# Queries, norms and keys of the next sample made inside the last window of the layer before, values made beside the first tiles

## The chip, the cores and the metric

The kernel runs on one core of a Trainium2 chip, in one launch. The metric is device time in microseconds, the median over several executions. All arithmetic is in float32, except a split of some operands into three bfloat16 parts. The engines are named as in the profile: PE is TensorE, DVE is VectorE, ACT is ScalarE, POOL is GpSimd, and SP is the engine that issues the DMAs.

## What is computed

Four layers run over x of 4 samples, 128 channels and 64 x 64 pixels. Layer 0, the only one whose arithmetic the change moves, is an attention over the 4096 pixels of one sample, cut here to what matters:

```python
x1 = conv1x1(x, v_w, v_b)                       # values
x2 = conv1x1(x, q_w, q_b)                       # queries
weight = conv1x1(leaky(conv1x1(x2, lw1)), lw2)  # one number per pixel
bias   = conv1x1(leaky(conv1x1(x2, bw1)), bw2)
# for each sample, q = queries, v = values as (C, n):
norm   = sqrt(sum(q * q, axis=0))
k      = q / clip(norm, 1e-4)                   # keys
logits = einsum('cn,cm->nm', k, q)
mean   = logits.mean(axis=0)
sparse = relu(logits - mean * weight + bias)
attn   = softmax(logits * sparse, axis=0)
attn   = clip(attn * (sparse != 0), 1e-8)
out    = einsum('cn,nm->cm', v, attn)
y      = leaky(conv3x3(out)) + x
```

Layer 1 projects its input, runs a selective scan over the 4096 pixels (64 states for each of 128 channels) beside a depthwise convolution, and adds the result to its input. Layer 2 is another attention with scalar queries and keys, and layer 3 a selective scan in both directions over all samples together, with a group norm behind it.

## The kernel before

The samples go one after the other: `layer0(b)`, then `layer1(b)`, for b from 0 to 3. Layer 2 of sample b - 1 is done in the gaps of both (`row_weights` beside layer 0, `attend` beside layer 1), only the last sample's layer 2 has a stage of its own; layer 3 comes last.

**Layer 0** has two parts. The first, lines 355 to 392, is a loop over 8 chunks of 512 pixels. Each chunk loads x, makes the queries on PE and ACT, stores them to DRAM (`self.q0`), squares them on POOL, sums the squares on PE in two layouts, takes the roots on ACT and stores the norms to DRAM, takes the inverse norms on DVE, spreads them over the partitions on PE (`inv_ps`), multiplies them with the queries into the keys `k`, sums the keys (`ksum`), and makes the values `vT` by four PE products and one DVE addition. The instructions of this loop are free for the scheduler to arrange. The mean of the keys follows, and `thresholds(0)`: four PE products one after the other with ACT and DVE steps between them, from the queries to the cut `ncut` and the bound `bound` of a block of 512 queries.

The second part, lines 591 to 637, is a loop over 128 tiles, 16 for each of the 8 blocks of queries. A tile makes 256 x 512 logits (`lg`) from keys and queries on PE; DVE adds the cut (`above`) and multiplies (`weights`), POOL subtracts the bound, ACT takes exp (`shifted`); masking is done on DVE for even tiles and on POOL for odd ones (`masked`). Eighteen tiles later (`LAG` = U + 2) the weights get their floor (`floored`) and meet the values (`product`), so the values aren't read in the first 18 tiles. Through `self.pinned()` every instruction of this part keeps its program order on its engine. Smaller jobs, the thresholds of the next block, the normalization and the convolution of finished blocks, are lists of steps in a `Queue`; each tile takes up to two of them and one that begins on PE.

**Layer 1** cuts the 4096 pixels in 4 windows of 1024. A window has 64 items (16 groups of 8 channels for each of 4 groups of states), so a sample has 256; all go through one `scan_stream`. An item loads a row of decays (`row<-d`, 512 KB broadcast from DRAM, asked for three items ahead), makes exp on ACT, spreads the driving term on PE, multiplies it on DVE, runs a scan on DVE and a product on POOL; four items later PE sums the products (`total`). Every fourth item has its driving term made on POOL instead. Beside the items, `side(k, n)` takes steps from a queue with `queue.tile`: one that begins on PE (not at every fourth item), and up to two others, where a step marked `on_dve` is held back till just before the next item's scan (`queue.late`). In windows 0 to 2 the queue holds the preparation of the next window (`prepared`: projection, norm, steps, with stores and loads over DRAM), in all windows the depthwise convolution of the window and the end of the window before it (`finish`). The end of the last window (`finish(3)`) runs after the last item: the last `total`, the output projection, the residual `res` and the first pass of layer 2.

Layer 0 of the next sample begins after this end: its first load waits until the last store of layer 1, `x2` from `res`, is over, since it takes the memory of layer 1's tiles.

Of the kernel before, what the change touches and what calls it, by code (L numbers as in the profile page):

```python
# [8 lines left out]
F32 = mybir.dt.float32  # L9
# [20 lines left out]
class Queue:  # L30
# [11 lines left out]
    def first(self, *runs):  # L42
        self.runs[:0] = [list(r) for r in runs]
# [72 lines left out]
class Net:  # L116


    def __init__(self, ctx, tc, ins, out):
# [178 lines left out]
    def weights12(self):  # L298
# [32 lines left out]
    def layer0(self, b):  # L331
# [8 lines left out]
        with self.pool("l0", 1) as big, self.pool("l0t", 2) as tmp, self.pool("l0a", LAG + 3) as ap, \  # L340
# [3 lines left out]
            ypad = self.padded_image(big, "ypad")  # L344
            ksum = big.tile([P, NCH], F32, name="ksum", tag="ksum")
            def misc(name, rows=P):
                return ps1.tile([rows, NB], F32, name=name, tag="misc")
# [6 lines left out]

            for c in range(NCH):
                s = bass.ts(c, NB)
# [45 lines left out]
            queue = Queue()  # L402
            held = {}
            qs, ncut, bound = {}, {}, {}

# [176 lines left out]
            beside = self.row_weights(b - 1, big, tmp) if b else lambda i: None  # L582
            queue.add(thresholds(0))
            queue.steps(1)
            if b == 0:
                self.weights12()
            logits(0)
            logits(1)
            above(0)
            due = {}  # L590
            for i in range(S + LAG + 2):
# [35 lines left out]
                if i < S and m == 1 and c + 1 < NCH:  # L627
                    queue.add(thresholds(c + 1))

# [231 lines left out]
    def layer1(self, b):  # L861
# [12 lines left out]
        with self.pool("l1", 1) as big, self.pool("l1c", 2) as work, self.pool("l1t", 2) as tmp, \  # L874
# [238 lines left out]
            def depthwise(w):  # L1113
# [31 lines left out]
                return steps  # L1145

            blocks, begins, runs = [], [], []
            for w in range(NW):
# [24 lines left out]
            def before(k, n):  # L1173
# [667 lines left out]
```

## Time and profile before

| | us |
|---|---|
| median of 3 runs | 10780.06 |
| lowest and highest of them | 10776.46, 10784.34 |
| profiled execution | 10792.41 |
| span of the profiled execution | 10790.6 |
| layer 0 tiles of the four samples, first to last e | 68.6 to 687.7, 1767.8 to 2407.8, 3505.9 to 4143.5, 5239.8 to 5877.3 |
| layer 1 items, first to last scan | 817.9 to 1681.0, 2535.7 to 3422.0, 4272.7 to 5157.5, 6005.2 to 6879.0 |
| layer 2 of the last sample begins | about 6891 |
| granted PE clock, mean | 0.893 |

Times inside the profiled execution count from the first instruction. A row of the timeline has the start, the duration, the engine, the line, the operation, output and inputs, and how many instructions were merged; in brackets stands how long the engine had been idle and what ended that. Line L111 is a helper through which all pinned instructions go, so those are told apart by their tiles. SPq rows are the issuing of DMAs. A row of the table by stretches has the stretch, its length, and for each engine the time that it was busy with the number of its instructions, then the granted PE clock, the busy share of the DMA engines and the rate that they moved.

### The profile page before, as it was taken

To read this page: it belongs to the slowest core of one execution; us is meant where nothing else is said; L and a number is where in the kernel's file an instruction comes from. 1 tells how busy PE (TensorE), PEld (TensorE's weight loads), DVE (VectorE), ACT (ScalarE), POOL (GpSimd) and SP (SyncE) were. 2 spreads that over 40 slices of the span, in tenths; PEclk is the share of its full clock that TensorE was granted. 3 is DMA by queue.
4 is the path that set the end of the run, shared out by engine and by line. 5 is a ranking of instruction groups with operands and counts; after the bars stand their busy time and mean duration, and the time that the engine had idled before them with its cause. 6 is when DMAs were issued, how large, how long until landed. Compare 5 with 4: busy or idle time off the path is not lost. (4 is left out here: it accounts for less than half of the span.)

```text
span 10790.6 us, 91073 instructions
## 1 busy us (share of the span) xinstructions
PE 8558.2 (79%) x28025; PEld 3043.4 (28%) x28104; DVE 9230.7 (86%) x6438; ACT 6291.6 (58%) x9435; POOL 8141.7 (75%) x3566
## 2 busy tenths in 40 slices
PE   8986667997877897877799778787777777777774
PEld 3331212332222333222233222332222222222221
DVE  7859996986997885999787799529999999999996
ACT  3324444664664664666465566556666666676764
POOL 6748886765886774888675688429999999998986
PEclk9997778998998998999899899889988898888887
DMA  1008772006885002788100788338888888888886
GB/s 29 15 20 195 191 191 58 12 15 149 206 201 147 10 15 68 198 204 201 40 17 12 176 210 198 94 73 205 197 208 196 209 198 209 208 225 224 223 218 179
DMA packets 502953, 1522.34 MB, mean 141 GB/s; under 512 B 83433, under 2 KB 91145, under 8 KB 502465
## 3 DMA queue, kind: packets, MB, share of 16 engines
q1 hardware_dynamic: 502464, 1516.51, 56.7%
q8 instruction: 223, 3.65, 0.2%
q14 instruction: 266, 2.17, 0.1%
HBM read 1327.38 MB, written 125.94 MB: 135 GB/s over the span
## 5 line engine op out<-in xcount | busy, mean ns | idle before, releaser
L111 POOL TENSOR_TENSOR p<-h,c_rep 128x1024 f32<-128x1024 f32 x2048 | 4807.3, 2357 | 818.6 <-DVE h L111 766.4
L111 DVE TENSOR_TENSOR_SCAN h<-da,carry,db 128x1024 f32<-128x1024 f32 x1536 | 3604.1, 2346 | 201.5 <-ACT da L111 22.4
L111 PE MATMUL db<-parts,sel 96*128 96x512 bf16 x4096 | 1404.9, 429 | 1546.6 <-DVE h L111 1527.4
L111 DVE TENSOR_TENSOR db<-b_rep,db 128x1024 f32<-128x1024 f32 x1536 | 1855.2, 1208 | 199.1 <-DMA b_rep<-bc 133.4
L111 ACT ACTIVATE da<-row,A 128x1024 f32<-128x1024 f32 x1536 | 1760.9, 1147 | 305.8 <-DMA row<-d 302.5
L111 POOL TENSOR_TENSOR e<-e,bound 128x1024 f32<-128x1024 f32 x512 | 1240.5, 2425 | 566.6 <-DVE e L111 566.4
L111 POOL TENSOR_TENSOR x<-row,b_rep 128x1024 f32<-128x1024 f32 x512 | 1209.1, 2362 | 151.8 <-DMA row<-d 151.0
L111 PE MATMUL total<-p,gather 128*32 128x512 f32 x8192 | 1256.5, 729 | 19.6 <-POOL p L111 19.6
L111 DVE TENSOR_TENSOR_SCAN h<-db,carry,x 128x1024 f32<-128x1024 f32 x512 | 1194.7, 2333 | 73.8 <-ACT db L111 43.7
L111 ACT ACTIVATE db<-db,A 128x1024 f32<-128x1024 f32 x512 | 555.5, 1085 | 1194.7 <-PE db L111 1139.7
L111 PEld LDWEIGHTS <-sel 96*128 96x128 bf16 x4096 | 307.3, 101 | 3119.9 <-DVE h L111 2151.6
L111 ACT ACTIVATE e<-e 128x1024 f32<-128x1024 f32 x512 | 541.0, 1057 | 1050.0 <-POOL e L111 1050.0
L111 PE MATMUL lg<-q,k 128*128 128x512 f32 x2048 | 1027.3, 626 | 153.1 <-DVE e L111 152.6
L111 PE MATMUL acc<-t,vT 128*128 128x512 f32 x2048 | 956.2, 594 | 6.4 <-DVE t L111 3.3
L111 PE MATMUL acc<-e,values 128*128 128x512 f32 x1536 | 856.2, 648 | 87.1 <-ACT e L111 61.5
L111 DVE TENSOR_TENSOR t<-lg,ncut 128x1024 f32<-128x1024 f32 x512 | 624.9, 1220 | 292.6 <-PE acc L111 260.7
L111 ACT ACT_TABLE_LOAD x593 | 760.8, 1283 | 39.5 <-DMA r<-y 18.9
L111 ACT COPY carry<-h 128x1 f32<-128x1 f32 x2048 | 374.6, 185 | 554.0 <-DVE h L111 549.8
L111 ACT ACTIVATE e<-gq,below,fcol 128x512 f32<-128x512 f32 x768 | 610.0, 805 | 94.8 <-PE acc L111 94.8
L111 POOL TENSOR_TENSOR t<-t,e 128x1024 f32<-128x1024 f32 x256 | 608.9, 2379 | 47.5 <-ACT t L111 45.9
L111 ACT ACTIVATE junk<-gp,ntop,fcol 128x512 f32<-128x512 f32 x768 | 619.5, 807 | 27.1 <-DMA gp<-g 14.4
L111 DVE SCALAR_TENSOR_TENSOR e<-t,lg 128x1024 f32<-128x1024 f32 x512 | 619.5, 1210 | 2.5
(214 smaller groups left out, 10007.9 us busy)
## 6 DMA issues: line engine op xcount, KB each, us to landing
row<-d SPq DMA_DIRECT2D x2048, 512.0 KB
parts<-split SPq DMA_DIRECT2D x960, 64.0 KB
b_rep<-bc SPq DMA_DIRECT2D x96, 512.0 KB
c_rep<-bc SPq DMA_DIRECT2D x96, 512.0 KB
d<-delta SPq DMA_DIRECT2D x80, 384.0 KB
r<-y SPq DMA_DIRECT2D x48, 512.0 KB
xq<-in_x SPq DMA_DIRECT2D x64, 256.0 KB
q<-q SPq DMA_DIRECT2D x64, 256.0 KB
```

The source lines that it names most:

```text
L111: return self.tc.keep_in_program_order(method(*args, **kwargs))
```

## The change

For samples 1 to 3 the first loop of layer 0 is gone. In its place `layer1(b)` for b < 3 gets a list of steps, `tokens(b + 1)`, which joins the queue when its last window begins. It works in 4 pieces of 1024 pixels: it loads x, makes queries and their squares on ACT from one PE product, the norms on PE and ACT, the inverse norms on DVE, the spreading on PE, the keys on DVE and the sums of the keys on ACT (`accum_out` into `self.ksum`, now a tile that lives through the whole kernel); queries, keys and norms are stored to DRAM, the keys into a new array `self.k0`. What is left in the queue at the last item is run there. It borrows layer 1's tiles: `delta` and `du` for queries, `res` for squares, `u` for keys, `split` for the small ones.

Layer 0 of samples 1 to 3 begins with the load of the first block's queries and norms, then 8 loads of keys, and the thresholds. Sample 0 keeps its first loop, without the values. The values of all samples become eight runs of three steps in the queue (`values`: load, four products, addition), taken in the first tiles; the thresholds of the second block go ahead of them. The weights `lin_wT` are asked for behind the first thresholds, and `W_inc` is made in place.

```diff
+        self.k0 = dram.tile([P, L], F32, name="k0", tag="k0")
+        self.ksum = self.const.tile([P, NCH], F32, name="ksum", tag="ksum")
-        self.W_inc = pool.tile([P, P], F32, name="W_inc", tag="W_inc")
+        self.W_inc = self.W_in[:, 0:P]
 # layer0
-            for c in range(NCH):
+            def key(c):
+                s = bass.ts(c, NB)
+                sp.dma_start(out=k[:, s], in_=self.k0[:, s])
+
+            for c in range(0 if b else NCH):
...
-                ps = misc("v_ps").rearrange("p (a b) -> p a b", b=P)
-                for i in range(4):
-                    nc.tensor.matmul(ps[:, i, :], xq[:, bass.ts(i, P)], self.v_wT, start=True, stop=True)
-                nc.vector.tensor_tensor(
-                    vT[:, 4 * c : 4 * c + 4, :], ps,
-                    self.v_b.unsqueeze(1).to_broadcast([P, 4, P]), ALU.add,
-                )
-            self.load_all(big, ["lin_wT"])
+            def values(c):
+                def load():
+                    held["xv"] = row("xq")
+                    sp.dma_start(out=held["xv"], in_=self.ins["x"][b, :, bass.ts(c, NB)])
+                def v():
+                    held["v"] = misc("v_ps").rearrange("p (a b) -> p a b", b=P)
+                    for i in range(4):
+                        pe.matmul(held["v"][:, i, :], held["xv"][:, bass.ts(i, P)], self.v_wT, start=True, stop=True)
+                def plus():
+                    dve.tensor_tensor(
+                        vT[:, 4 * c : 4 * c + 4, :], held["v"], self.v_b.unsqueeze(1).to_broadcast([P, 4, P]), ALU.add,
+                    )
+                return [load, on_pe(v), plus]
...
             queue.add(thresholds(0))
+            if b:
+                queue.step()
+                for c in range(NCH):
+                    key(c)
             queue.steps(1)
+            self.load_all(big, ["lin_wT"])
...
+            for c in range(NCH):
+                queue.add(values(c))
             logits(0)
...
-                    queue.add(thresholds(c + 1))
+                    (queue.add if c else queue.first)(thresholds(c + 1))
 # layer1
+            def tokens(b):
+                M = W // P
+                held, small = {}, []
+                def load(u):
+                    held["x", u] = work.tile([P, W], F32, name="x", tag="x")
+                    sp.dma_start(out=held["x", u], in_=self.ins["x"][b, :, bass.ts(u, W)])
+                def first():
+                    small.append(tmp.tile([P, 3, NB], F32, name="split", tag="split", bufs=1))
+                    load(0)
+                def a(u, c):
+                    def go():
+                        held["ps"] = misc("q_ps")
+                        pe.matmul(held["ps"], self.q_wT, held["x", u][:, bass.ts(c, NB)], start=True, stop=True)
+                    return on_pe(go)
+                def query(u, c):
...
+                        act.activation(held["q", u][:, s], held["ps"], AF.Identity, bias=self.q_b)
+                        act.activation(held["sq"][:, s], held["ps"], AF.Square, bias=self.q_b)
+                def squares(u):
...
+                                held["ps"][:, i : i + 1], held["sq"][:, bass.ts(i, P)], self.ones[:, 0:1],
...
+                def root(u):
+                    def go():
+                        act.activation(norm(u), held["ps"][:, 0:M], AF.Sqrt)
+                        self.exp_tables(act)
+                    return go
+                def inverted(u):
+                    def go():
+                        dve.tensor_scalar(inverse(u), norm(u), 1e-4, None, ALU.max)
+                        dve.reciprocal(inverse(u), inverse(u))
+                    return go
+                def turned(u):
...
+                        pe.matmul(held["ps"][:, 0:P], norm(u), self.ident, start=True, stop=True)
+                def kept(u):
+                    return lambda: act.copy(as_rows(u), held["ps"][:, 0:P])
+                def spread(u, c):
...
+                def key(u, c):
...
+                        dve.tensor_tensor(held["k", u][:, s], held["ps"], held["q", u][:, s], ALU.mult)
+                    return on_dve(go)
+                def store(u):
+                    def go():
+                        t = bass.ts(u, W)
+                        sp.dma_start(out=self.q0[:, t], in_=held["q", u])
+                        sp.dma_start(out=self.k0[:, t], in_=held["k", u])
+                        sp.dma_start(out=self.norms[:, t].rearrange("o (i p) -> (o i) p", p=P), in_=as_rows(u))
+                    return go
+                def sums(u):
...
+                            act.activation(
+                                small[0][:, 2, :], held["k", u][:, bass.ts(c, NB)], AF.Identity,
+                                accum_out=self.ksum[:, u * C + c : u * C + c + 1],
+                            )
+                steps = []
+                for u in range(NW + 1):
+                    if u < NW:
+                        beside = ([sums(u - 2)] if u > 1 else []) + ([lambda u=u: load(u + 1)] if u + 1 < NW else [])
+                        steps += [a(u, 0), query(u, 0), then(*beside), a(u, 1), query(u, 1)]
+                    else:
+                        steps += [sums(u - 2)]
+                    if u:
+                        steps += [inverted(u - 1), turned(u - 1), kept(u - 1)]
+                        for c in range(C):
+                            steps += [spread(u - 1, c), key(u - 1, c)]
+                    if u < NW:
+                        steps += [squares(u), root(u)]
+                    if u:
+                        steps += [store(u - 1)]
+                return first, steps + [sums(NW - 1)]
...
                     queue.add(image(w) + depthwise(w))
+                    if w == NW - 1 and not last:
+                        first, steps = tokens(b + 1)
+                        first()
+                        queue.add(steps)
                 queue.tile(i % 4 != 1)
+                if i == NW * SG * G - 1:
+                    queue.late()
+                    while queue:
+                        queue.step()
```

More of the change, by code (lines that the diff above doesn't have):

```diff
@@ L344, in layer0 @@
             ypad = self.padded_image(big, "ypad")
-            ksum = big.tile([P, NCH], F32, name="ksum", tag="ksum")
+            ksum = self.ksum
             def misc(name, rows=P):
@@ L1145, in depthwise, with norm, inverse, as_rows @@
                 return steps
+            def tokens(b):
[14 more added lines that the diff above has]
+                    def go():
+                        s = bass.ts(c, NB)
+                        if c == 0:
+                            held["q", u] = scratch(("delta", "du")[u % 2])
+                            held["sq"] = scratch("res")
+                        act.activation(held["q", u][:, s], held["ps"], AF.Identity, bias=self.q_b)
[3 more added lines that the diff above has]
+                    def go():
+                        held["ps"] = misc("n_ps")
+                        for i in range(M):
+                            pe.matmul(
+                                held["ps"][:, i : i + 1], held["sq"][:, bass.ts(i, P)], self.ones[:, 0:1],
+                                start=True, stop=True,
+                            )
+                    return on_pe(go)
+                def norm(u):
+                    return small[0][:, 0, 2 * u * M : (2 * u + 1) * M]
+                def inverse(u):
+                    return small[0][:, 0, (2 * u + 1) * M : (2 * u + 2) * M]
+                def as_rows(u):
+                    return small[0][0:M, 1, bass.ts(u, P)]
+                def root(u):
[4 more added lines that the diff above has]
+                def inverted(u):
+                    def go():
+                        dve.tensor_scalar(inverse(u), norm(u), 1e-4, None, ALU.max)
+                        dve.reciprocal(inverse(u), inverse(u))
+                    return go
+                def turned(u):
+                    def go():
+                        held["ps"] = misc("t_ps", M)
+                        pe.matmul(held["ps"][:, 0:P], norm(u), self.ident, start=True, stop=True)
+                    return on_pe(go)
+                def kept(u):
+                    return lambda: act.copy(as_rows(u), held["ps"][:, 0:P])
+                def spread(u, c):
+                    def go():
+                        held["ps"] = misc("i_ps")
+                        for i in range(NB // P):
+                            pe.matmul(
+                                held["ps"][:, bass.ts(i, P)],
+                                inverse(u)[:, c * NB // P + i : c * NB // P + i + 1].to_broadcast([P, P]),
+                                self.ident, start=True, stop=True,
+                            )
+                    return on_pe(go)
+                def key(u, c):
+                    def go():
+                        s = bass.ts(c, NB)
+                        if c == 0:
+                            held["k", u] = work.tile([P, W], F32, name="u", tag="u")
+                        dve.tensor_tensor(held["k", u][:, s], held["ps"], held["q", u][:, s], ALU.mult)
+                    return on_dve(go)
+                def store(u):
+                    def go():
+                        t = bass.ts(u, W)
+                        sp.dma_start(out=self.q0[:, t], in_=held["q", u])
+                        sp.dma_start(out=self.k0[:, t], in_=held["k", u])
+                        sp.dma_start(out=self.norms[:, t].rearrange("o (i p) -> (o i) p", p=P), in_=as_rows(u))
+                    return go
+                def sums(u):
+                    def go():
+                        for c in range(C):
+                            act.activation(
+                                small[0][:, 2, :], held["k", u][:, bass.ts(c, NB)], AF.Identity,
+                                accum_out=self.ksum[:, u * C + c : u * C + c + 1],
+                            )
+                    return go
+                def then(*fs):
+                    def go():
+                        for f in fs:
+                            f()
+                    return go
+                steps = []
[7 more added lines that the diff above has]
+                        steps += [inverted(u - 1), turned(u - 1), kept(u - 1)]
+                        for c in range(C):
+                            steps += [spread(u - 1, c), key(u - 1, c)]
[4 more added lines that the diff above has]
+                return first, steps + [sums(NW - 1)]
```

## The prediction

> **What bounds the kernel now.** I read the page's engine rows first, to see that no single engine fills the span; then the timeline at the three joints where layer 1 of one sample hands over to layer 0 of the next; then the table by stretches, to see what bounds the two places that receive the moved work; then single timeline rows for the price of what is new. The chain of waits on the page is empty here, so the path is read from the timeline.
>
> ```profile
> span 10790.6 us, 91073 instructions
> PE 8558.2 (79%) x28025; PEld 3043.4 (28%) x28104; DVE 9230.7 (86%) x6438; ACT 6291.6 (58%) x9435; POOL 8141.7 (75%) x3566
> ```
>
> The time is a string of stages with different limits; VectorE at 86% is a mean over them. The joint before the second sample:
>
> ```profile
> 1703.16 0.42 SPq L111 DMA_DIRECT2D x<-res  x1
> 1705.97 0.81 SPq L358 DMA_DIRECT2D xq<-in_x  x2
> 1709.25 2.04 PE L360 MATMUL lg<-xq,q_wT 128*128 128x512 f32 x2 [6.95 <-DMA xq<-in_x]
> 1752.68 1.59 PE L111 MATMUL th_ps<-q,w_T 128*64 128x512 f32 x2 [0.86 <-DMA q<-q]
> 1762.71 5.69 PE L111 MATMUL lg<-q,k 128*128 128x512 f32 x8
> ```
>
> Line 1 stores layer 1's last piece, line 2 loads x for the new sample as soon as that store is over, line 3 is the first query product. For 43 us the queries, norms, keys and values are made with nothing beside them (line 4 ends that), then the threshold chain runs, and the attention tiles begin on line 5. The same distance from line 3 to line 5 is 53.46 us here, 52.16 at the next joint (3448.99 to 3501.15) and 52.19 at the last (5182.74 to 5234.93): 157.8 us in all. Stretches (layer-1 windows 1, 2 and 3 of the second sample, and above them the first 16 tiles of its layer 0):
>
> ```profile
> core 0: us, PE busy (x) PEld busy (x) DVE busy (x) ACT busy (x) POOL busy (x), PEclk, DMA share, GB/s
> 1767.80:1842.00 74.20, 50.97 (x130) 14.98 (x128) 57.67 (x43) 48.44 (x84) 59.04 (x24) 0.88 0.00 0
> 2759.30:2981.50 222.20, 179.73 (x646) 64.28 (x646) 215.60 (x137) 149.11 (x228) 188.82 (x82) 0.91 0.83 207
> 2981.50:3207.60 226.10, 180.25 (x661) 65.42 (x661) 215.89 (x137) 153.92 (x235) 188.96 (x82) 0.95 0.81 200
> 3207.60:3424.40 216.80, 161.06 (x559) 50.12 (x558) 210.79 (x132) 118.68 (x187) 185.36 (x81) 0.86 0.71 176
> ```
>
> The last window, where the new work goes, has room on ScalarE, TensorE and the DMA queue, but VectorE is busy 210.8 of 216.8 us: what is added there on VectorE is paid. The first tiles have 16 us free on VectorE out of 74, but as gaps in a chain.
>
> **Part 1, taken off the joints.** At the joint the changed program loads queries, norm rows and keys from DRAM and goes straight to the threshold chain; the means of the keys come from sums held in SBUF. The first load can start where line 2 starts, since the same store of layer 1 is awaited. I let the chain's first product begin where the first query product begins now. The chain then costs 10.0 us at this joint (1752.68 to 1762.71) and 8.8 at the last. Here a rule weighs in: the Trainium skill, "TensorE: Matmul & The Clock Gate", Part 1, says that TensorE halves its clock after about 3.4 us of idleness and needs as much work to get it back. The removed products are what kept it warm. The first sample shows a chain that is cold all through:
>
> ```profile
> 53.36 1.97 PE L111 MATMUL th_ps<-q,w_T 128*64 128x512 f32 x2
> 61.77 2.07 PE L111 MATMUL th_ps<-h,bw_rep 64*128 64x512 f32 x2 [0.84 <-DVE m L111]
> ```
>
> From 53.36 to the first tile product at 63.77 it is 10.4 us. By the rows of the joints themselves the gain would be 157.8 - (10.0 + 8.8 + 8.8) = 130.2; by the rule and the cold row 157.8 - 3 x 10.4 = 126.6. I take **-126.6** (bounds -134 and -118). The key loads are 8 x 256 KB; only the first is needed by the first tile, the others at two tiles each (9.5 us), so they hide behind the tiles; lin_wT is loaded at 1694.82 before and stays near there.
>
> **Part 2, added to three last windows.** Per window, with durations of like rows:
> - VectorE: 8 key products like k<-inv_ps,q at 0.69: 5.5 us. 4 reciprocals of 0.18: 0.7. 4 clamps of 128x8 (tensor_scalar, SBUF to SBUF): 0.16 each when alone, but see below.
> - ScalarE: 8 x (0.69 + 0.60) for queries and squares, 8 x (0.69 + 0.19) for the sums, 4 roots of 0.27 with two table loads of 1.28, 4 small copies: 30 us.
> - TensorE: 8 query products as pairs (8 x 1.0), 32 of the norm, 32 of the spreading at 0.25 to 0.29, 4 turns: 26 us.
> - SP and DMA: 4 loads of 512 KB, 8 stores of 512 KB and 4 of 4 KB: 6.3 MB on the 38 MB that pass now (176 GB/s by 216.8 us), so 205 GB/s, what windows 1 and 2 carry.
>
> ScalarE would reach 149, TensorE about 187: windows 1 and 2 run with as much and take 222 to 226. So these engines are bounded by a row, and the window should become a little worse than those, by what VectorE has more. The clamp's price:
>
> ```profile
> 2841.42 0.66 DVE L111 TENSOR_TENSOR u<-u,rs_ps 128x512 f32<-128x512 f32 x1
> 2841.64 2.35 POOL L111 TENSOR_TENSOR p<-h,c_rep 128x1024 f32<-128x1024 f32 x1 [1.25 <-DVE h L111]
> 2842.12 2.43 DVE L111 TENSOR_SCALAR u<-u,gamma,beta 128x1024 f32<-128x1024 f32 x1
> ```
>
> The tensor_scalar takes 2.43 where it takes 0.81 with GpSimd idle (776.62), and ends just after GpSimd's product; a PSUM source (first row) isn't touched. "GPSIMD Engine Reference", 1. Specifications, has the rule: GpSimd shares its SBUF interfaces with VectorE and collides with two-port or two-input instructions. By the short row alone the 4 clamps cost 0.6; by rule and row up to 4 x 1.8 = 7.2. The clamp stands right after a scan, when GpSimd is often just free, so I take 1.0 each, 4.0. VectorE: 5.5 + 0.7 + 4.0 = 10.2. Windows with side work also idle more (6.6 and 10.2 against 6.0): +2.3. So 12.5 a window, **+37.5** for three (bounds 21 and 56).
>
> A second rule speaks against the roots: "ScalarE: Activation LUTs", What ACT_TABLE_LOAD costs, gives 2.66 us a switch, a drain included, thus 5.3 for root and back. The trace has load 2827.65, root 2828.95, load 2829.23, next work 2830.53: 2.9 us with no drain to be seen. The rule would add 11 us of ScalarE a window, 160 of 229: still not the bound, nothing in the sum.
>
> **Part 3, the end of layer 1.** The queue is drained at the last item. In the changed order only the last turn, two spreads, two key products, the three stores and two pairs of sums are left there. They lie in VectorE's 6.25 us wait for the last total. But the residual load res<-x, issued at 1657.48 now, comes behind the last key store on SP, some 3.7 us after the last scan's end; with an estimated 4 us to land (the x store's 2.8 and the keys ahead) it meets its use 9.6 us after that end. On one PSUM bank the second spread waits for the first key product and holds the last totals back by about half a microsecond. +1 each, **+3** (0 to 9).
>
> **Part 4, values beside the first tiles.** 32 loads move into SP's order behind the keys, 32 VectorE additions of 0.69 and 128 products move into the tiles. In samples two to four a pair of tiles takes 9.5 us (starts of e<-t,lg 2.45 and 7.05 apart), chained from VectorE's e through GpSimd and ScalarE's exp back to VectorE's masking; an addition stands after each masking, so it lengthens the chain by up to 8 x 0.69 = 5.5 us a sample, or nothing where it falls in a wait. I take 5: **+15** (0 to 17). The first v product is queued behind six tile products; 2.75 MB stand before its x, 14 us at 200 GB/s, landing at 1722 against its turn at about 1727: hidden, 1 us each for each microsecond later.
> In the first sample the value products leave the prologue (5.4 us a chunk; without the 0.7 of v products and the addition before the clamp an estimated 4.5): -7. The weights' loads hold SP there (21.6 us for the A_log pieces), so tile products queue behind the first value load; with the additions +5. **-2** (-8 to +6).
>
> Sum: -126.6 + 37.5 + 3 + 15 - 2 = -73.1. The profiled execution took 10792.4 (span 10790.6 and 1.8 around it), 12.4 above the median of 10780.1; on the median's base 10707, in a profile about 10719.
>
> **The rivals.**
> - Cheap landing (14%): additions and clamps fall into waits. Windows +7 each, values 0, tail 0: -126.6 + 21 - 7 = -113, 10667. Against it: VectorE idles only 6 us in the window.
> - Late start (15%): loads or the drain lie in the way after all; 8 us a joint for a v product stuck behind slow key loads (98 GB/s was the mean of the old prologue), or for the residual. -73 + 24 = -49, 10731. Against it: the store of line 1 moved 512 KB within 2.8 us.
> - Slower (3%): the key store waits on SP for VectorE, and the row<-d loads are queued behind it. A row is asked for three items, 10 us, ahead; when a store holds SP longer than that lead less the landing, ScalarE's decay and the scan stop. 12 stores lose the whole gain at 73 / 12 = 6.1 us each; at 8 us the time is 10803. Against it: the store's step comes a full tile after its key product; in windows 1 and 2 of the third sample row loads were waited for only 2.4 us, beside as many bytes.
> - The work is moved and nothing gained (3%): the joint's wait is the store of line 1 and a chain as long as before; 10780. Against it: lines 3 to 5.
> - The forecast has the other 65%.
>
> The range 10668 to 10742 takes the forecast with its bounds, most of the cheap case and the late start. Under 0.2% (21.6 us) is about what a measurement of this kernel can't tell from no change. Faster 0.94, within it 0.03, slower 0.03.
>
> **What would show it.** Right: about 10.4 us from the first th_ps to the first lg at each joint, th_ps starting some 6 us after the x store; last windows of 225 to 230 us with VectorE near 221; the first 16 tiles about 5 us longer; clamps between 0.2 and 2.4. Wrong: a joint above 20 us, a last window above 236, SP waiting in a key store with a row wait behind it, or first tiles no longer than now.

## The result, and the profile after

The changed kernel takes 10659.3 us (median of 5 runs, 10649.1 to 10665.2) against 10779.1 for the kernel before (5 runs, 10776.3 to 10784.3): ratio 0.9888, 95% interval 0.9873 to 0.9902. It is faster by 120 us where the prediction said 73, and lies 9 us below the lower end of the range. The direction was right, the size wrong.

The page's head, to compare with the head shown before:

```profile
span 10662.4 us, 91085 instructions
PE 8514.6 (80%) x28080; PEld 3044.8 (29%) x28080; DVE 9216.5 (86%) x6390; ACT 6331.1 (59%) x9504; POOL 8117.2 (76%) x3542
```

Nothing in it shows where 120 us went, since the shares moved by a point at most. The joint before the second sample does (timeline; start, duration, engine, line, operation):

```profile
1703.12 0.42 SPq L111 DMA_DIRECT2D x<-res  x1
1705.90 0.32 SPq L111 DMA_DIRECT2D q<-q  x1
...
1708.82 1.94 PE L111 MATMUL th_ps<-q,w_T 128*64 128x512 f32 x2 [6.55 <-DMA own<-norms]
...
1719.32 2.93 PE L111 MATMUL lg<-q,k 128*128 128x512 f32 x3
```

The store of layer 1's last piece is followed at once by the load of the queries, and the threshold chain starts 5.7 us after the store was issued. Before, that store was followed by 43 us of queries, norms, keys and values. (The wait is put down to the norms' load, issued 0.4 us behind that of the queries; the product reads the queries.) The chain itself takes 10.50 us.

The stretches that the prediction rested on, after the change (the second sample's first 16 tiles, then its layer-1 windows 1 to 3, counted from 0):

```profile
core 0: us, PE busy (x) PEld busy (x) DVE busy (x) ACT busy (x) POOL busy (x), PEclk, DMA share, GB/s
1724.00:1797.30 73.30, 55.28 (x194) 22.20 (x192) 63.41 (x52) 48.45 (x84) 59.10 (x24) 0.93 0.07 22
2712.40:2936.10 223.70, 178.11 (x647) 62.66 (x646) 215.82 (x137) 148.77 (x228) 188.98 (x82) 0.93 0.83 206
2936.10:3162.10 226.00, 184.22 (x661) 66.64 (x660) 216.14 (x138) 152.96 (x236) 189.24 (x82) 0.92 0.81 200
3162.10:3382.40 220.30, 172.48 (x699) 68.79 (x698) 215.56 (x147) 143.55 (x232) 185.56 (x81) 0.93 0.78 197
```

In the first row VectorE carries 5.7 us more than before (63.41 against 57.67), yet the 16 tiles are no longer (73.30 against 74.20, and 72.60 in a second profile of the kernel before). In the last row VectorE carries 4.8 us more (215.56 against 210.79), and the window is 3.5 us longer.

Stage by stage, from the starts of the same instructions in each trace. The third column is a second profile of the kernel before, the first experiment below. Sums over samples, in us:

| stage | before | before, again | after | after less before | forecast |
|---|---|---|---|---|---|
| three joints, last scan's end to first tile product | 231.2 | 233.2 | 99.7 | -131.5 | -123.6 (parts 1 and 3) |
| three last windows | 645.6 | 645.6 | 659.1 | +13.5 | +37.5 (part 2) |
| first 16 tiles, samples 2 to 4 | 219.5 | 217.9 | 219.1 | -0.3 | +15 (part 4) |
| first sample up to its 16th tile | 135.2 | 135.2 | 136.3 | +1.1 | -2 (part 4) |
| layer 0's last tile to layer 1's first scan | 515.1 | 507.2 | 505.9 | -9.2 | 0 |

The first four rows give -117.2, close to the 119.8 between the medians. The last row looked like a gain that nobody had foreseen; it isn't one.

### The profile page after: what moved, and what is told of

It reads as the page before. It is cut to its first block, busy times and chain, and to the rows that moved or that the text cites. A ratio compares the mean times of both kernels' runs of the same rounds, so it can differ in the third digit from the quotient of the medians.

```text
span 10662.4 us, 91085 instructions
## 1 busy us (share of the span) xinstructions
PE 8514.6 (80%) x28080; PEld 3044.8 (29%) x28080; DVE 9216.5 (86%) x6390; ACT 6331.1 (59%) x9504; POOL 8117.2 (76%) x3542
## 5 line engine op out<-in xcount | busy, mean ns | idle before, releaser
L111 PE MATMUL total<-p,gather 128*32 128x512 f32 x8192 | 1251.2, 730 | 10.4 <-POOL p L111 10.2
L111 ACT ACT_TABLE_LOAD x617 | 791.6, 1283 | 38.9 <-DMA r<-y 17.6
```

What stands on the lines that cost most here:

```text
L111: return self.tc.keep_in_program_order(method(*args, **kwargs))
```

## The experiments

**The kernel before, profiled again.**

> The kernel before, unchanged, for a second profile. It tells how much one stage differs between two profiles of the same program. Theory A (the stretch from layer 0's last tile to layer 1's first scan, 124 to 128 us in the changed kernel and 127.8 to 130.2 in the one before, is shorter by 1.5 to 3.9 us a sample only because TensorE's granted clock fell otherwise in that execution): at least two of the four stretches move by 1 us or more, some below 127. Theory B (the change shortens it): all four within 0.5 us of 130.2, 127.8, 129.2 and 127.9. The last windows (213.5, 216.7, 215.4, 215.1) should move by less than 1.5 us, the joints (79.4, 76.8, 75.1 from the last scan's end to the first tile product) by less than 1. Time ratio 1.000.

Span 10772.5 us against 10790.6 in the first profile, ratio 1.0007 (0.9998 to 1.0015). The stretch of the last row moves by 7.9 us in sum between two profiles of one program; in the changed kernel TensorE's granted clock from 90 to 110 us behind the last tile of the fourth sample is 0.74, in the first profile of before 0.59. So the -9.2 is mostly the spread between executions. Theory A holds, and differences of some 8 us in that row mean nothing: over the 14 profiles of all runs it lies between 497.2 and 515.1. The last windows repeat within 1.4 us each, the joints within 1.3.

The runs below leave most stages of the changed kernel as they are, and so show how much a stage varies from one execution to the next. Unaltered, the joints give 98.3 to 100.4 (4 profiles), the last windows 659.1 to 663.5 (5), the first 16 tiles of samples 2 to 4 219.1 to 223.1 (5), and the first sample up to its 16th tile 133.7 to 136.4 (5). So the row of the joints is firm, that of the last windows is +13.5 to +18, and the two rows of the first tiles can't be told from nothing. Within a last window VectorE's busy time repeats to 0.4 us. Its idle time does so only in the first sample (4.7 to 5.1); in the second and third it goes from 4.5 to 7.1 in the changed kernel and from 4.7 to 6.3 before.

**Are VectorE's additions in the last window paid?** Each key product is issued twice.

```diff
                 dve.tensor_tensor(held["k", u][:, s], held["ps"], held["q", u][:, s], ALU.mult)
+                dve.tensor_tensor(held["k", u][:, s], held["ps"], held["q", u][:, s], ALU.mult)
```

> The changed kernel with each of the 24 moved key products on VectorE (0.67 us) issued twice. Theory A (the forecast's: what is added to VectorE in the last window is paid at its row duration or more, with more idle time): the three last windows grow by 5 us or more each, +15 to +20 in all. Theory B (VectorE is one closed chain there; an added instruction is paid at its step from start to start, and nothing else comes with it): 7 more in the window at 0.55 to 0.6, so +3.9 to +4.2 a window, +12 in all, idle time unchanged at about 4.7. Theory C (the additions fall into waits): below +1 a window. Against the kernel before: 0.9888 in theory C, 0.990 in B, 0.9905 in A; the windows in the profile decide, not the ratio.

The three last windows:

```profile
1456.20:1678.80 222.60, 150.06 (x604) 55.41 (x604) 217.63 (x149) 107.33 (x177) 185.34 (x81) 0.79 0.72 183
3149.60:3375.40 225.80, 176.68 (x699) 69.87 (x698) 219.83 (x153) 143.39 (x231) 185.84 (x81) 0.91 0.76 192
4858.10:5084.70 226.60, 184.01 (x699) 72.37 (x698) 219.62 (x153) 143.46 (x231) 185.88 (x81) 0.87 0.75 191
```

They are 4.4, 5.5 and 6.0 us longer than in the changed kernel (218.2, 220.3, 220.6). Six more products stand in each, and VectorE is busy 3.9 to 4.3 us more, 0.7 each; the rest is idle time of 0.2, 1.2 and 2.1 us. The ratio is 0.9907 (0.9892 to 0.9921). Theory C falls: these additions find no wait. B has the busy time right. The added idle time that A foresaw is not shown: the 5.0, 6.0 and 7.0 us here lie within what unaltered windows have.

**What does the clamp cost?** Clamp and reciprocal are put one place later.

```diff
                 dve.reciprocal(inverse(u), inverse(u))
-            return go
+            return on_dve(go)
```

> The changed kernel with the clamp and the reciprocal put one place later on VectorE: not right behind a scan but behind the next item's product db<-b_rep,db. Theory A (the clamp, SBUF to SBUF, cannot go on while GpSimd's product runs, and was cheap, 0.15 to 0.38 us, only because it stood in the gap of 0.3 us between two GpSimd products): it now takes 0.9 to 2.2 us each, ending with GpSimd's product, and the last windows grow by about 1 us for each of the 3 or 4 clamps in them, 2 to 5 us a window. Theory B (a clamp of 8 columns is cheap wherever it stands): 0.15 to 0.4 each, windows within 1 us of 218.2, 220.3 and 220.6.

Timeline of the changed kernel, then of this one, at the same clamp:

```profile
3324.20 2.33 DVE L111 TENSOR_TENSOR_SCAN h<-db,carry,x 128x1024 f32<-128x1024 f32 x1
3324.43 4.67 POOL L111 TENSOR_TENSOR p<-h,c_rep 128x1024 f32<-128x1024 f32 x2 [1.26 <-DVE h L111]
3326.44 0.38 DVE L111 TENSOR_SCALAR split<-split 128x8 f32<-128x8 f32 x1
3326.85 0.20 DVE L111 RECIPROCAL split<-split 128x8 f32<-128x8 f32 x1
```

```profile
3332.06 1.21 DVE L111 TENSOR_TENSOR db<-b_rep,db 128x1024 f32<-128x1024 f32 x1
3332.36 2.35 POOL L111 TENSOR_TENSOR p<-h,c_rep 128x1024 f32<-128x1024 f32 x1
3333.18 1.57 DVE L111 TENSOR_SCALAR split<-split 128x8 f32<-128x8 f32 x1
3334.67 2.35 POOL L111 TENSOR_TENSOR x<-row,b_rep 128x1024 f32<-128x1024 f32 x1
3334.78 0.20 DVE L111 RECIPROCAL split<-split 128x8 f32<-128x8 f32 x1
```

Below, the clamp starts amid GpSimd's product and ends with it (3334.75 against 3334.71); above, it starts as one GpSimd product has 0.35 us to go (the row merges two; the first ends at 3326.79) and slips through before the next. Over the twelve clamps it is 0.15 to 0.38 us above and 1.42 to 1.57 below. The last windows grow by 4.1, 4.6 and 6.7 us, of which VectorE's busy time is 4.4, 4.7 and 4.6; the ratio is 0.9908 (0.9893 to 0.9923). Theory A holds: the price belongs to the place. The product db<-b_rep,db, which reads PSUM, isn't touched in the same lines (1.21 us; 1.207 is its mean).

**Are the value additions paid?** Each is issued twice.

```diff
                 dve.tensor_tensor(
                     vT[:, 4 * c : 4 * c + 4, :], held["v"], self.v_b.unsqueeze(1).to_broadcast([P, 4, P]), ALU.add,
                 )
+                dve.tensor_tensor(
+                    vT[:, 4 * c : 4 * c + 4, :], held["v"], self.v_b.unsqueeze(1).to_broadcast([P, 4, P]), ALU.add,
+                )
```

> The changed kernel with each of the 32 moved value additions on VectorE (0.68 us) issued twice. Theory A (the forecast's: an addition after each masking lengthens the chain of a pair of tiles): the first 16 tiles of a sample grow by 8 x 0.6 = about 5 us, +19 in all. Theory B (GpSimd and the waits around it set the pair's 9.51 us, and the addition fills time in which VectorE would have waited or been held up): 73.3, 72.6 and 73.3 us of samples 2 to 4 stay within 0.7, and a pair of tiles stays at 9.5 us. Ratio to the kernel before 0.9905 in A, 0.9888 in B.

Samples 2 to 4 take 74.4, 73.3 and 73.3 us (73.3, 72.6, 73.3 without), and a pair of tiles stays at 9.51 to 9.53 us: theory B there, with one value 1.1 us up instead of 0.7, which unaltered runs show too (74.9). In the first sample a pair goes from 7.96 to 8.39 us, and the 16 tiles from 71.1 to 78.1. So the additions aren't free everywhere. Three such pairs make 1.3 of those 7 us. Another 3.0 lie around one late threshold step (TensorE waits 2.69 us for ScalarE's m); the run with the values alone has that step late by as much in its first sample (2.5 us) with no addition doubled, so it can't be put down to them. The cause of that, and of the rest, is open. The ratio is 0.9890 (0.9874 to 0.9907).

**What does set the pair?** One of ScalarE's two row-weight exponentials per tile is issued twice in the first 16 tiles.

```diff
-            act.activation(junk, g[0], AF.Exp, ...)
+            for _ in range(2 if i < 16 and u % 2 == 0 else 1):
+                act.activation(junk, g[0], AF.Exp, ...)
```

> The changed kernel with one of the two row-weight exponentials on ScalarE (junk<-gp, 0.80 us and 0.19 for its sum) issued twice in each of the first 16 tiles of samples two to four. Theory A (a pair of tiles goes round between GpSimd and ScalarE, 9.51 us, and VectorE stands outside of that ring, so that the doubled value additions cost nothing): the pair grows by 1 to 2 us, the first 16 tiles by 6 to 15 us a sample. Theory B (VectorE's masking and products set the pair): within 1 us of 73.3, 72.6 and 73.3.

In the one execution of this run the pair is 10.45 us instead of 9.51 and the 16 tiles 78.8 us in each of samples 2 to 4: +17.2 in sum. That is 0.94 for the pair and 5.5 to 6.2 for a sample, just under theory A's ranges and far from B; of two added ScalarE steps of 0.99 us a pair, one lies on the ring. The ring, in the changed kernel's timeline (GpSimd and ScalarE rows and VectorE's masking of one pair):

```profile
3458.85 0.81 ACT L111 ACTIVATE junk<-gp,ntop,fcol 128x512 f32<-128x512 f32 x1
3459.66 1.04 ACT L111 ACTIVATE t<-t 128x1024 f32<-128x1024 f32 x1
3460.61 1.04 ACT L111 ACTIVATE e<-e 128x1024 f32<-128x1024 f32 x1
3460.78 2.36 POOL L111 TENSOR_TENSOR t<-t,e 128x1024 f32<-128x1024 f32 x1 [1.51 <-ACT t L111]
3461.68 2.55 DVE L111 SCALAR_TENSOR_TENSOR t<-t,e 128x1024 f32<-128x1024 f32 x1 [1.25 <-ACT e L111]
3463.10 3.34 POOL L111 TENSOR_TENSOR e<-e,bound 128x1024 f32<-128x1024 f32 x1
3464.15 0.68 DVE L111 TENSOR_TENSOR vT<-v_ps,v_b 128x512 f32<-128x512 f32 x1
3466.40 2.37 POOL L111 TENSOR_TENSOR e<-e,bound 128x1024 f32<-128x1024 f32 x1
```

GpSimd waits 1.51 us for ScalarE's t, which stands behind the row-weight exponential; then GpSimd runs its three products in a row, and ScalarE's next exponential (3466.48) waits for the second of them. VectorE's e and its addition aren't on the ring: its e for the next tile was ready at 3459.29, 3.8 us before GpSimd took it up at 3463.10, and even the other e of the pair, made behind the addition (3464.75, 1.20 us), is ready some 0.4 us before GpSimd's last product of the row begins. That product isn't on the ring either: it ends at 3468.77, and ScalarE takes its result at 3470.12. The addition takes slack, and the wait of 1.25 us ahead of the masking shows that VectorE has it. The masking itself may be on the ring: the GpSimd product that begins beside it takes 3.34 us, the like one behind it 2.37. That the masking holds it up was not tested.

**The values alone.** The kernel before with only the values moved.

> The kernel before with only the values moved beside the first tiles; queries, norms and keys are made at the joint as before. By the theory that the additions stand in waits of the tiles (first 16 tiles of samples two to four longer by under 1 us), the gain is what leaves the four prologues: about 0.7 us of products and additions for each of 8 chunks where they set the pace; the first sample's prologue became 3.3 us shorter in the changed kernel. So each joint 2.5 to 4 us shorter, the first sample's tiles 4.5 us longer from the late load: -5 to -10 us, ratio 0.9990 to 0.9995. By the forecast's own terms (+5 a sample in the tiles) it would be no gain or a loss of up to 10.

A miss: 10778.5 against 10773.4 us, ratio 1.0004 (0.9996 to 1.0013). The joints are 237.9 us in sum, longer than before, not shorter. Four chunks of queries and keys with the values beside them (before), and without them (this kernel):

```profile
3463.20:3481.60 18.40, 18.35 (x111) 12.48 (x112) 8.51 (x20) 5.47 (x12) 3.13 (x4) 1.00 0.31 102
```

```profile
3453.20:3471.90 18.70, 16.74 (x80) 9.27 (x80) 10.20 (x16) 5.38 (x13) 4.15 (x4) 1.00 0.25 87
```

A chunk takes 4.68 us before and 4.66 here (query products at 42.78, 47.46 and 52.15 us behind the last scan before, at 43.35, 48.01 and 52.66 here). TensorE shows busy all the time in the first row, and taking 1.14 us of value products out of each chunk changes nothing. In this kernel TensorE waits in the first joint 3.2 us for GpSimd's square and 3.0 for VectorE's reciprocal (0.9 and 1.5 before); that these hand-overs set the pace is how I read it, no run tests it. Without the values the threshold chain is slower (31.1 us in sum against 27.6). So moving the values alone is worth nothing; the gain comes with the queries, norms and keys. What these would bring with the values left at the joint was not run.

**Why did the end of layer 1 not get longer?** The kernel before with spare products at its last item.

```diff
                 queue.tile(i % 4 != 1)
+                if i == NW * SG * G - 1 and not last:
+                    while queue:
+                        queue.step()
+                    for _ in range(2):
+                        ps = misc("i_ps")
+                        for m in range(NB // P):
+                            pe.matmul(ps[:, bass.ts(m, P)], self.ones, self.ident, start=True, stop=True)
```

> The kernel before with 8 spare TensorE products (128x128, result unused) at the last item of layer 1 of the first three samples, where the changed kernel has the drained products of the keys. Theory A (these products keep TensorE's clock up, which is why the end of layer 1 got shorter and not longer in the changed kernel): the four output products after the last scan take 2.0 instead of 3.8 us, and the first query product comes about 2 us sooner after the last scan's end (25.9, 24.6 and 22.9 now), -4 to -6 us in all. Theory B (the 2 us come from another order of the stores): distances as before within 0.7.

The output products behind the last scan: before, with the spare products, and in the changed kernel, where the drained spreads of the keys stand ahead of them.

```profile
3431.89 3.78 PE L111 MATMUL o_ps<-xc,W_out 128*128 128x512 f32 x4 [1.31 <-DVE xc L111]
```

```profile
3406.67 2.27 PE L111 MATMUL i_ps<-ident,ones 128*128 128x128 f32 x16
...
3417.31 1.98 PE L111 MATMUL o_ps<-xc,W_out 128*128 128x512 f32 x4 [1.31 <-DVE xc L111]
```

```profile
3383.03 1.16 PE L111 MATMUL i_ps<-ident,split 128*128 128x128 f32 x8 [1.99 <-DVE u L111]
...
3389.66 1.98 PE L111 MATMUL o_ps<-xc,W_out 128*128 128x512 f32 x4 [1.31 <-DVE xc L111]
```

With the spare products the first query product comes 22.2, 21.2 and 21.1 us behind the last scan, not 25.9, 24.6 and 22.9: -9.0 in all, more than theory A's -4 to -6, because the last totals quicken too (o_ps starts 5.8 us behind the scan, not 7.5). The queue that the edit drains was empty: the traces differ in these products alone. The granted clock over o_ps is 0.50 in the first of the three fences and 1.00 in the other two. Chance has a part: in the third joint of the kernel before o_ps took 1.98 without help (3.78 at all three in the second profile), and in one joint of the run with the queries kept it took 3.67 in spite of the drained spreads. The time falls by too little for a verdict (0.9994, 0.9987 to 1.0001).

**Is the chain at the joint slow for the clock?** The changed kernel with 16 spare products in TensorE's wait for the queries.

```diff
                 for c in range(NCH):
                     key(c)
+                for _ in range(4):
+                    ps = misc("w_ps")
+                    for m in range(NB // P):
+                        pe.matmul(ps[:, bass.ts(m, P)], self.ones, self.ident, start=True, stop=True)
```

> The changed kernel with 16 spare TensorE products (128x128, result unused) ahead of the threshold chain of samples two to four, in the 5.4 us in which TensorE waits for the queries from DRAM. Theory A (the chain of 10.50 us runs on a clock that went down in that wait): the chain falls to about 8.8 us, what it was behind the query and value products in the kernel before, -1.7 us a joint, -5 in all. Theory B (the chain's length comes from the hand-overs between engines): 10.3 to 10.5 as now. If the spare products last longer than the wait, the chain starts later by the difference.

The third joint, with them:

```profile
5084.48 4.70 PE L111 MATMUL w_ps<-ident,ones 128*128 128x128 f32 x32
5090.56 1.04 PE L111 MATMUL th_ps<-q,w_T 128*64 128x512 f32 x2 [1.38 <-issue]
5092.50 1.12 PE L111 MATMUL th_ps<-q,kbar_rep 128*128 128x512 f32 x2 [0.90 <-ACT h L111]
5094.30 1.12 PE L111 MATMUL th_ps<-h,lw_rep 64*128 64x512 f32 x2 [0.68 <-ACT m L111]
5096.27 1.12 PE L111 MATMUL th_ps<-h,bw_rep 64*128 64x512 f32 x2 [0.84 <-DVE m L111]
```

The chain is 6.76 us here, 8.30 at the second joint, and still 10.50 at the first. The stretches of the chain at the first joint of the changed kernel and at the third here have granted clocks (third figure from the end) of 0.50 and 1.00:

```profile
1708.80:1719.30 10.50, 8.06 (x8) 1.77 (x8) 0.75 (x1) 1.27 (x2) 0.00 (x0) 0.50 0.88 304
```

```profile
5090.50:5097.30 6.80, 4.32 (x8) 1.08 (x8) 0.75 (x1) 1.27 (x2) 0.00 (x0) 1.00 0.99 353
```

At the second joint it is 0.75. So the clock is worth up to 3.7 us of the chain. Ratio 0.9882 (0.9867 to 0.9897), not apart from the changed kernel's.

Why only one of three joints stays fast can be read from the clock's own record. In all 14 profiles the granted clock is 0.50 or 1.00, and its changes (over 600 in each) lie whole multiples of 3.41 us apart, all but one in a hundred of them to 0.002 us. So it moves only at the ends of fixed slots of 3.41 us. In this run it fell at the end of these slots, one for each joint:

```profile
1697.60:1701.01 3.41, 1.61 (x13) 1.23 (x11) 1.64 (x9) 0.00 (x0) 0.00 (x0) 1.00 0.45 148
3400.85:3404.26 3.41, 1.84 (x4) 0.59 (x4) 0.00 (x0) 1.27 (x2) 0.00 (x0) 1.00 0.89 295
5093.86:5097.27 3.41, 2.12 (x4) 0.59 (x4) 0.75 (x1) 0.39 (x1) 0.00 (x0) 1.00 1.04 389
```

That is just ahead of the chain at the first joint, in its third product at the second, and as it ended at the third. Once down, the clock came back only behind slots in which TensorE was at least 79% busy (all 4381 rises of the 14 profiles, with the ends of products as the profile models them); the slots of the first joint's chain are 62 to 80% busy, 2.11 to 2.74 us, and it stayed at 0.50. Falls mostly follow emptier slots (under 77% busy in 95% of them), but a slot of 1.76 us at the second joint let the clock stay up, so the busy share alone does not decide a fall.

**The first sample's late load.** x for the first values is loaded ahead of the later layers' weights.

```diff
+            runs = [values(c) for c in range(NCH)]
             if b == 0:
+                runs[0].pop(0)()
                 self.weights12()
-            for c in range(NCH):
-                queue.add(values(c))
+            for run in runs:
+                queue.add(run)
```

> The changed kernel with the first sample's first load of x for the values issued ahead of the weights of the later layers, not behind them. In the changed kernel TensorE stands 7.3 us in the first tiles (68.5 to 75.8), waiting for that load, which is issued at 72.40 when the A_log pieces are through. Theory A (that wait is paid): the first 16 tiles of the first sample go from 71.1 to about 66.5 us, the time falls by 4 to 5 us. Theory B (the next loads behind the weights, q and own norms of the second chunk at 72.86 and 73.28, hold the tiles as long): 70 to 71 us, nothing gained. Other samples unchanged.

The first value product in the changed kernel and here:

```profile
75.78 2.04 PE L111 MATMUL v_ps<-v_wT,xq 128*128 128x128 f32 x8 [7.32 <-DMA xq<-in_x]
```

```profile
68.33 1.05 PE L111 MATMUL v_ps<-v_wT,xq 128*128 128x128 f32 x8
```

The 7.32 us wait is gone, and the 16 tiles take 67.0 us, not 71.1: theory A. The ratio, 0.9882 (0.9866 to 0.9899), is not apart from the changed kernel's.

**The first queries kept in SBUF.**

```diff
                 act.activation(held["q", u][:, s], held["ps"], AF.Identity, bias=self.q_b)
+                if u == 0 and c == 0:
+                    act.activation(self.q_first, held["ps"], AF.Identity, bias=self.q_b)
...
-                qs[c] = held["q"] = row("q")
-                sp.dma_start(out=qs[c], in_=self.q0[:, s])
+                if b and c == 0:
+                    qs[c] = held["q"] = self.q_first
+                else:
+                    qs[c] = held["q"] = row("q")
+                    sp.dma_start(out=qs[c], in_=self.q0[:, s])
```

> The changed kernel with the first 512 queries of the next sample kept in SBUF by one more ScalarE copy of 0.69 us in the last window, so that the joint loads no queries before its threshold chain; for room the mean column is 1 wide, and two replicated weight columns are read with stride 0. Theory A (the load of the queries, issued behind the last store of layer 1 and landing about 3 us later, is what the joint ends on): the chain starts about 4 us sooner after the last scan's end (23.5, 22.2 and 22.5 now), so -12 us in all, and up to 1.7 us more a joint where TensorE's clock is then still up; the time falls by 0.11 to 0.16%. Theory B (the release of layer 1's buffers behind its last stores is what it ends on): the chain starts within 1 us of now.

The chain starts 18.5, 16.7 and 16.6 us behind the last scan's end, 5.0 to 5.9 us sooner; the joints are 82.1 us in sum, -17.6. Theory A. Ratio 0.9873 (0.9859 to 0.9888).

**Both together, without and with spare products in the chain.**

> Two edits of the runs before together on the changed kernel: the first 512 queries of the next sample stay in SBUF, and the first sample's first load of x for the values is issued ahead of the later layers' weights. If each keeps its gain (17.6 us at the three joints, 4.1 in the first tiles, both read from stages), the time falls by 20 to 22 us below the changed kernel's, 10630 to 10640 us, ratio to the kernel before 0.987. If the gains are taken back later (other stages vary by some 8 us in sum from one profile to the next), 10650.

> The same two edits, and 22 spare TensorE products (128x128, result unused) in the waits of the threshold chain of samples two to four: 14 behind its first product, 4 behind the second, 4 behind the third. Theory A (the last two products of the chain, 1.1 to 2.1 us each in the run with the queries kept, are long because TensorE's clock falls in the waits between them): all four take about 1.1, and the way from the first product to the first tile product (11.74, 9.49, 9.15) shortens by about 1.2 us each. Theory B (the hand-overs set it, and the spare products stand in the way): unchanged or longer by up to 1 us.

Without: 10638.8 us against 10773.4 for the kernel before on the same chip, ratio 0.9874 (0.9857 to 0.9890). By stages against the changed kernel the joints give -18.3 and the first sample -4.2; the last windows take back 3.9, which is within their spread. The intervals of the two ratios overlap, so the stages, not the ratio, say that it is the faster of the two. Its second joint:

```profile
3380.53 1.07 PE L111 MATMUL th_ps<-q_first,w_T 128*64 128x512 f32 x2
3381.46 0.42 SPq L111 DMA_DIRECT2D x<-res  x1
3383.09 0.68 ACT L111 ACTIVATE h<-th_ps,w_b 64x512 f32<-64x512 f32 x1 [1.96 <-DMA h<-values]
3383.92 1.10 PE L111 MATMUL th_ps<-q_first,kbar_rep 128*128 128x512 f32 x2 [2.33 <-DVE kbar_rep L176]
```

The chain now starts ahead of layer 1's last store; its second step waits for layer 1's store of the values, whose memory h seems to take. With the spare products all four products take 1.0 to 1.1 us as theory A says, but the 14 behind the first one last 3.4 us, past that wait: the chain takes 10.48, 9.27 and 9.27 us against 12.47, 8.46 and 8.98. Ratio 0.9879 (0.9864 to 0.9893): nothing gained.

## Why the prediction was wrong, point by point

Most of the error lies in two terms that were sized far too high: the last windows (part 2, by 24 us) and the values beside the tiles (part 4, by 15). Parts 1 and 3 together gave 8 us more than forecast.

- **Part 1, the joints (-126.6): right.** The chain was put at 10.4 us on a cold clock and took 10.50 three times; the trace's rows of the joints themselves (10.0, 8.8, 8.8) would have been 3.9 us too good in sum. The granted clock over the chain was 0.50 three times, against 0.52, 0.69 and 0.70 at the joints before, so the removed products had kept it up only in part. The rule that the prediction took from the Trainium skill, "TensorE: Matmul & The Clock Gate", Part 1, with a cold chain at each joint, was the better guide here, and the run with spare products shows the clock as the cause.
- **Part 3, the end of layer 1 (+3): wrong in sign.** Joint and end together gave -131.5 where -123.6 stood. The step that failed is "+1 each": it counted what the drained steps hold up, and not that their products keep TensorE's clock up for what follows. The chain started 2.4, 2.4 and 0.4 us sooner behind the last scan than the first query product had, not 1 later. Of these 5.2 us, o_ps makes 3.6: 1.98 us at all three joints instead of 3.78, 3.78 and 1.98. That spare products suffice for this is shown in the kernel before.
- **Part 2, the last windows (+37.5): a third to a half of it, +13.5 in this profile and up to +18 in others.** That VectorE is paid is right (the doubled key products). The terms of one window were: key products 5.5, reciprocals 0.7, clamps 4.0, more idle time 2.3. Measured in the second sample's window: clamps 1.0 in sum, a mean of 0.26 and not 1.0; six key products, 4.0, since the seventh starts with the last scan's end and the eighth lies in VectorE's wait behind it, which part 3 had said itself; reciprocals 0.8. These 5.8 us of rows became 4.8 of busy time (215.56 less 210.79), because the start of one VectorE row overlaps the end of the one before. Idle time is 4.7, 4.7 and 4.9 us in the three windows, against 5.0, 5.9 and 4.7 before (the 5.9 with one wait of 1.2 for o_ps). Over the five profiles with unaltered windows its mean is 4.8, 5.6 and 6.2, over the four of windows without the new work 5.0, 5.7 and 5.3: not +2.3 a window but some 0.2. Three sizes failed, then: the clamp, the number of key products, and the idle time. For the last, windows 1 and 2 idle longer and have side work, and I let the last one follow them.
- **Part 4, the values (+15): nothing, -0.3.** The failed step is "chained from VectorE's e through GpSimd and ScalarE's exp back to VectorE's masking". VectorE's two e of a pair are ready 3.8 and 0.4 us before GpSimd takes them; the ring runs between GpSimd and ScalarE (the doubled exponential), with VectorE's masking in it at most, and in samples 2 to 4 the addition takes VectorE's slack (the doubled additions). The upper bound had been taken nearly whole.
- **Part 4, the first sample (-2): +1.1 in this profile, -1.5 to +1.2 over five.** So the term is not refuted. The prologue gave 3.5 us, the late load took 4.6; the load alone costs 4.1, as the run with the earlier load shows.
- **What would have shown it wrong:** "first tiles no longer than now" is what the trace shows.
- **The rivals.** The cheap landing (10667) came nearest, with its windows at +7 and values at 0; but in the windows nothing fell into waits, the additions were smaller. The slower case did not come: VectorE's longest wait in a last window is 0.5 us (1.6 in other profiles).
- **The base.** The profiled execution of before (10792.4 us) lies 13 us above the median, that of the changed kernel (10664.2) 5 above its own, so the 128 us between the two profiles overstate the 120 between the medians.

## What to carry to other kernels

Before an addition is priced as lengthening a chain, follow one turn of the chain in the timeline and ask of each engine how long its output lies before the next one takes it: VectorE's e on the ring lay 3.8 us, so 0.68 us more there cost nothing, while on ScalarE, whose output GpSimd stood waiting for, 0.99 us cost 0.94. A small instruction that another engine can hold up is priced by the place it will stand in, which can be read beforehand: here 0.15 to 0.38 us at the seam between two GpSimd products and 1.4 to 1.6 inside one. Ahead of crediting a removal, ask whether the engine that looks full sets the pace: the joint's TensorE showed over 99% busy, and 1.14 us less for it in each chunk of 4.68 was worth nothing.

## What the runs showed that I had not expected

- TensorE products that nobody needs made a following stage shorter: 8 of them at the end of layer 1 brought the next stage 9.0 us closer over three joints.
- TensorE's granted clock changes only at the ends of fixed slots of 3.41 us. Behind the same spare products the chain took 6.76, 8.30 or 10.50 us by where it lay against these slots: the waits of TensorE ahead of it were 1.38, 0.91 and 2.15 us, in another order.
- Two profiles of one program differ by 18 us in span, 7.9 of it in one stretch where the granted clock varies, and VectorE's idle time in one unaltered window goes from 4.5 to 7.1 us.
